# A landing margin for transfers in the planner's model, two more tiles for rows of B, one fewer for the scan states

## The chip, the cores and the metric

The kernel runs on one core of one Trainium2 chip. The metric is the device time of one execution in microseconds. The core has five engines that matter here, each with its own instruction queue, worked off in order: PE (matmuls and transposes), ACT (activations), DVE (vector operations, the scans among them), POOL (elementwise products here) and SP, which issues every transfer between memory and the on-chip buffer.

## The reference, cut to what matters

Eight images of 56 x 56 positions and 192 channels pass through two residual layers. The first is an attention with depthwise convolutions; it is the "front" of an image in the kernel, together with the convolution that opens the second layer. The second layer is a selective scan in four directions (rows and columns, each forward and backward). Its core, with A, B, C and the step size d computed from the image:

```
def step(h, inp):
    u_l, d_l, B_l, C_l = inp
    dA = jnp.exp(d_l[..., None] * A)
    dBu = d_l[..., None] * B_l[:, :, None, :] * u_l[..., None]
    h = dA * h + dBu
    y = jnp.sum(h * C_l[:, :, None, :], axis=-1)
    return (h, y)
```

There are 384 channels (three blocks of 128 partitions, NJ = 3), 16 states per channel (n = 0 to 15) and 3136 positions. The four results are added, normalized, gated and projected, and the image is added back.

## The kernel before

A *chunk* is 448 positions of one direction of one image: 7 chunks a direction, 28 a batch (an image), 224 in all. Per chunk and per state n the engines do this:

- SP loads row n of B, broadcast over 128 partitions, into a tile `bb` (L1111, L1112). The ring of such tiles has three (pool `s3`). For the states in BY_POOL it also loads the row of C into a tile `cb` (L1115), of which there are two.
- POOL multiplies `du` (step size times input, one tile for a chunk, made at L1089) by the row into a state tile `h` of 3 x 448 columns (L1126). The ring of `h` tiles has HBUFS = 8.
- ACT makes the decays `da` (L1140), one per block. DVE scans in place in `h` (L1157), three scans, and copies the last column to `newc` (L1179), from which the next chunk goes on.
- For 11 of the 16 states (13 in the last batch) PE turns `h` (L1203), ACT scales it by C on the way out (L1219), and PE turns it back and adds it up in the PSUM tile `y` (L1237). For the others POOL multiplies by the row of C (L1256), adds pairs (L1260) into the one tile `yp`, and PE adds that to `y` (L1275). DVE adds the finished `y` to the sum of directions, `yacc` (L1290, L1292).
- Before a chunk, `prepared` loads the step-size rows and the inputs and makes the step sizes `dl_s` on PE, ACT and DVE (L1066 to L1085), then `du_s` on POOL (L1089).

Beside the scan of image b run the front of image b + 1, its projections (`x_proj`) and, at the start of a batch, the `finish` of image b - 1. At that point the skip loads (L1102) refill `yacc`.

The order of the instructions on each engine is written by a planner when the program is built. Every piece of work is a generator that yields requests: an engine, a cost in us, the cells it reads and those it writes, and for a transfer a fifth number, the time from issue to landing. The class `Sched` keeps a clock for each engine, gives each time the request that can start first (less a rank), and records when its result will be there. The plan decides nothing on the chip but the order of each queue; there, an engine waits until its next instruction's inputs are there. A ring hands out its tiles in turn: `Ring.ready` says whether the next one has been released by all requests of its last user, and the last reader's planned end is taken over as the earliest time at which it may be written. Where PE would stand still by the plan for more than 2 x T_FILL, `keep_busy` puts in a small matmul on zeros (L1371, T_FILL = 0.225 us of planned time each).

The requests of a row load and of the product that uses it:

```
bb = yield s3("bb", [128, T])
yield from dma([m["k_rows"][k, c]], bb.c, 3.2, bb.ap, ...)
...
h = yield sh("h", [128, NJ, T], parts=1 + 2 * NJ)
yield POOL, t_pool(NJ * T), bb.c + du.c[1:], [h.c[0]]
nc.gpsimd.tensor_tensor(h.ap, du.ap, bb.ap.unsqueeze(1)..., ALU.mult)
```

`row_loads` is one generator: when it waits for a `cb` tile, the `bb` loads after it wait too.

Of the kernel before, what the change touches and what calls it, by code (L numbers as in the profile page):

```python
# [21 lines left out]
T = 448  # L22
# [19 lines left out]
BY_POOL = (((2, 7), (12,)), ((2, 5), (8, 10), (13,)))  # L42
EPS = 1e-5
CAP = 60.0
HBUFS = 8
LEAD = 3


# [5 lines left out]
PE, ACT, DVE, POOL, SP = range(5)  # L54
LATE = (0.17, 0.08, 0.09, 0.06, 0.0)
HOP = 0.04
URGENT = 0.4


# [104 lines left out]
class Sched:  # L164
# [37 lines left out]
    def give(self, s, t):  # L202

        e, cost, reads, writes = s.req[:4]
        end = t + cost
        self.at[e] = end
        self.used[e] += cost
        if s.group is not None and e == PE:
            self.spent[s.group] = self.spent.get(s.group, 0.0) + cost
        end = t + s.req[4] if len(s.req) > 4 else end + LATE[e]  # L210
        for c in reads:
            c.r = max(c.r, end)
        for c in writes:
            c.w = end
        s.end = max(s.end, end)
        self.resume(s)

    def run(self, until=None):
        while True:
# [20 lines left out]
            for s in self.stages:  # L240
# [3 lines left out]
                if s.group in self.limit:  # L244
# [4 lines left out]
                    if spent < must:  # L249
                        rank = URGENT  # L250
                e, _, reads, writes = s.req[:4]
# [6 lines left out]
                else:  # L258
                    for c in writes:
                        if c.r > t:  # L260
                            t = c.r
                    t = max(t + HOP, self.at[e])
                    if best is None or t - rank < best[0]:
# [9 lines left out]
def kernel(  # L273
# [93 lines left out]
    for nm, src in (("q", bn_q), ("kv", bn_kv)):  # L367
        p = load(f"bn{nm}", [CP, 4, NB], src.rearrange("v (b p) -> p v b", p=CP))
        s = const.tile([CP, NB], F32, name=f"bns{nm}")
        t = const.tile([CP, NB], F32, name=f"bnt{nm}")  # L370
# [30 lines left out]
    s3 = Rings(ctx.enter_context(tc.tile_pool(name="s3", bufs=3)), 3)  # L401
    sh = Rings(ctx.enter_context(tc.tile_pool(name="sh", bufs=HBUFS)), HBUFS)
    c1 = Rings(ctx.enter_context(tc.tile_pool(name="c1", bufs=1)), 1)
# [61 lines left out]
    def dma(reads, writes, late, dst, src, after=()):  # L465
        yield SP, 0.07, reads, writes, late
        nc.sync.dma_start(dst, src)
        for t in after:
            t.free()
# [563 lines left out]
    for i in range(2):  # L1033
        t = keep.tile([128, T], F32, name=f"dts{i}")
# [70 lines left out]
    def row_loads():  # L1105
        for i, n in todo:
            b, k, c, _ = steps[i]
            yield lambda: i in chunks
            m = made[b]
            cols = slice(c * T, (c + 1) * T)  # L1110
            bb = yield s3("bb", [128, T])  # L1111
            yield from dma([m["k_rows"][k, c]], bb.c, 3.2, bb.ap, m["rows"][k][R + n, cols].partition_broadcast(128))  # L1112
            brow[i, n] = bb
            if n in by[i]:
                cbr = yield s2("cb", [128, T])  # L1115
                yield from dma([m["k_rows"][k, c]], cbr.c, 3.2, cbr.ap,
                               m["rows"][k][R + NST + n, cols].partition_broadcast(128))
                crow[i, n] = cbr
# [178 lines left out]
    with tc.manual_schedule():  # L1297
# [11 lines left out]
        with ExitStack() as es:  # L1309
# [16 lines left out]
            for rank, g in enumerate((prepared, skips, row_loads, inputs_made, decays, scans, carries, turned, scaled,  # L1326
                                      by_pool, back, summed, evicted)):
                sc.spawn(g(), 0.3 + 0.01 * rank, "scan")
# [114 lines left out]
```

## Time and profile before

| | |
|---|---|
| median of 3 runs | 18,865.54 us (18,856.12 to 18,895.47) |
| the profiled execution: own time, span | 18,891.11 us, 18,889.4 us |
| busy share of the span | PE 90%, ACT 78%, DVE 77%, POOL 87% |
| products of du and rows of B on POOL (L1126) | 3584, 3.05 us each |
| scans on DVE (L1157) | 10,752, 1.08 to 1.14 us each |
| filler matmuls on PE (L1371) | 11,944 records, 1651 us busy |
| mean granted TensorE clock | 0.971 of full speed |

A profile is one execution. A row of it names the line of the kernel, the engine, the operation and the tiles written and read, then busy time, the mean of one, and the idle time of the engine just before these instructions with what ended it. Idle time is set down to the instruction, or the transfer, whose semaphore came last. The records of PE's matmuls are pipelined and overlap, so its busy share overstates its load. A filler matmul of the plan is two records in the profile.

### The profile page before, as it was taken

How to read it: one execution, taken by the hardware profiler on the slowest of the kernel's cores; microseconds unless marked ns; L12 is line 12 of the kernel's file. 1: busy time of each engine (PE TensorE's matmuls, PEld its weight loads, DVE VectorE, ACT ScalarE, POOL GpSimd, SP SyncE). 2: the span in 40 equal slices, each digit the busy share in tenths (PEclk: the TensorE clock that was granted, in tenths of full speed). 3: DMA queues.
4: the chain of work that ended last, by engine and by line, in shares of the span. 5: the costliest groups of instructions: out<-in, count | busy, mean ns of one | idle time of the engine just before them, and what ended most of it. 6: DMA issues, size and time to landing. Idle time of an engine off the chain costs nothing. (4 is left out here: it accounts for less than half of the span.)

```text
span 18889.4 us, 274433 instructions
## 1 busy us (share of the span) xinstructions
PE 16973.1 (90%) x96640; PEld 11599.8 (61%) x96640; DVE 14534.5 (77%) x19156; ACT 14643.6 (78%) x26598; POOL 16416.5 (87%) x7528
## 2 busy tenths in 40 slices
PE   8789998999889998899898998889988899988888
PEld 4465566666666656665666655666556665666776
DVE  2387877887778777787777877778777788778887
ACT  2378877787777878778787887878778788888888
POOL 0388998899989999899998999989999899999997
PEclk9899999999999999999999999999999999999999
DMA  1332334323333333322333333332333333342222
GB/s 52 111 89 82 96 96 120 82 85 92 104 112 84 83 95 104 112 84 81 105 100 107 83 84 101 104 106 83 83 96 110 100 83 86 100 120 76 78 78 64
DMA packets 1128347, 1750.79 MB, mean 93 GB/s; under 512 B 168516, under 2 KB 1110840, under 8 KB 1123896
## 3 DMA queue, kind: packets, MB, share of 16 engines
q1 hardware_dynamic: 1126968, 1733.23, 32.2%
q8 instruction: 764, 12.52, 0.3%
q14 instruction: 615, 5.04, 0.1%
HBM read 1545.05 MB, written 187.74 MB: 92 GB/s over the span
## 5 line engine op out<-in xcount | busy, mean ns | idle before, releaser
L1157 DVE TENSOR_TENSOR_SCAN h<-da,newc,h 128x448 f32<-128x448 f32 x9216 | 10111.4, 1136 | 2166.1 <-ACT da L1140 1155.7
L1126 POOL TENSOR_TENSOR h<-du_s,bb 128x1344 f32<-128x1344 f32 x3584 | 10836.0, 3050 | 280.5 <-DMA bb<-rows 246.0
L1140 ACT ACTIVATE da<-dl_s,acoef 128x448 f32<-128x448 f32 x10752 | 6762.2, 636 | 1149.4 <-DVE h L1157 968.0
L1219 ACT ACTIVATE g<-ht,ct_s 112x384 f32<-112x384 f32 x10080 | 5663.7, 576 | 1776.0 <-PE ht L1203 1701.2
L1237 PE MATMUL y<-ident,g 112*128 112x112 f32 x30240 | 4742.3, 271 | 660.2 <-ACT g L1219 506.3
L1237 PEld LDWEIGHTS y<-ident,g 112*128 112x128 f32 x30240 | 3305.9, 143 | 3236.8 <-ACT g L1219 2466.3
L1203 PE MATMUL ht<-ident,h 128*112 128x128 f32 x30240 | 4935.7, 277 | 287.4 <-DVE h L1157 87.4
L1203 PEld LDWEIGHTS ht<-ident,h 128*112 128x112 f32 x30240 | 3481.3, 135 | 1064.4 <-issue 450.9
L1256 POOL TENSOR_TENSOR yp<-h,cb 128x448 f32<-128x448 f32 x1932 | 2147.0, 1143 | 454.8 <-PE y L1275 216.6
L1157 DVE TENSOR_TENSOR_SCAN h<-da,h 128x448 f32<-128x448 f32 x1536 | 1598.9, 1077 | 406.0 <-ACT da L1140 214.3
L1089 POOL TENSOR_TENSOR du_s<-dl_s,du_s 128x1344 f32<-128x1344 f32 x224 | 682.6, 3047 | 1338.5 <-DVE dl_s L1085 1300.8
L1256 POOL TENSOR_TENSOR h<-h,cb 128x448 f32<-128x448 f32 x1260 | 1399.1, 1141 | 291.3 <-issue 175.6
L1371 PE MATMUL y<-zeros 128*128 128x64 f32 x11944 | 1651.3, 272 | 0.0
L1371 PEld LDWEIGHTS y<-zeros 128*128 128x128 f32 x11944 | 1586.1, 198 | 48.6 <-issue 48.6
L1275 PE MATMUL y<-yp,ident 128*128 128x448 f32 x3864 | 1594.0, 547 | 5.1 <-POOL yp L1260 4.5
L453 PE MATMUL bank<-xa,dg 128*128 128x440 f32 (+2 forms) x3024 | 1318.4, 543 | 89.0 <-ACT g L1219 52.2
L1260 POOL TENSOR_TENSOR yp<-yp,h 128x1344 f32<-128x1344 f32 x420 | 1280.9, 3050 | 1.6
L757 PE MATMUL bank<-qT,kT 128*112 128x448 f32 x2352 | 1101.8, 559 | 83.8 <-ACT pT L707 47.2
L766 PE MATMUL bank<-pT,vt 112*128 112x448 f32 x2352 | 1002.1, 546 | 66.8 <-ACT pT L707 43.4
L1275 PEld LDWEIGHTS y<-yp,ident 128*128 128x128 f32 x3864 | 701.3, 193 | 551.6 <-issue 505.2
L453 PE MATMUL bank<-band,dgq 96*96 96x440 f32 (+3 forms) x2016 | 860.9, 544 | 54.4 <-ACT hq L583 29.9
L707 ACT ACTIVATE pT<-bank,nsh 112x448 f32<-112x448 f32 x1176 | 744.3, 635 | 172.9 <-PE bank L757 152.5
(152 smaller groups left out, 12958.1 us busy)
## 6 DMA issues: line engine op xcount, KB each, us to landing
bb<-rows SPq DMA_DIRECT2D x3584, 224.0 KB
cb<-rows SPq DMA_DIRECT2D x1064, 224.0 KB
xt<-x1d SPq DMA_DIRECT2D x224, 336.0 KB
du_s<-xch SPq DMA_DIRECT2D x112, 672.0 KB
du_s<-xcw SPq DMA_DIRECT2D x112, 672.0 KB
xch<-xv SPq DMA_DIRECT2D x24, 1568.0 KB
xcw<-xw SPq DMA_DIRECT2D x168, 224.0 KB
xs<-xch SPq DMA_DIRECT2D x56, 672.0 KB
```

The costliest lines, as they stand in the source:

```text
L453: nc.tensor.matmul(out[:, o0:o1, a:b], lhs, img(lo, hi)[:, :, a + dx - 1:b + dx - 1], start=(t == TAPS[0]), stop=(t == TAPS[-1]))
L757: nc.tensor.matmul(ps.ap[:TP, :T], kts[h][:, kb * TP:(kb + 1) * TP], qh.ap, start=True, stop=True)
L1126: nc.gpsimd.tensor_tensor(h.ap, du.ap, bb.ap.unsqueeze(1).to_broadcast([128, NJ, T]), ALU.mult)
L1140: nc.scalar.activation(da.ap[:, :T], dl.ap[:, j], AF.Exp, scale=acoef[:, k * NJ + j, n:n + 1])
L1157: nc.vector.tensor_tensor_scan(h.ap[:, j, rev], da.ap[:, 0:T][:, rev], h.ap[:, j, rev], news[i - 1].ap[:, j, n:n + 1] if ci else 0.0, ALU. ...
L1203: nc.tensor.transpose(ht.ap[:TP, j * 128:(j + 1) * 128], h.ap[:, j, s * TP:(s + 1) * TP], ident)
L1219: nc.scalar.activation(g.ap, ht.ap[:TP, :DIN], AF.Copy, scale=ct.ap[:, s, n:n + 1])
L1237: nc.tensor.matmul(y["t"].ap[:, j, s * TP:(s + 1) * TP], g.ap[:, j * 128:(j + 1) * 128], ident[:TP, :TP], is_transpose=True, start=(n == 0 ...
L1256: nc.gpsimd.tensor_tensor(to.ap[:, j], h.ap[:, j], cbr.ap, ALU.mult)
L1260: nc.gpsimd.tensor_tensor(yp.ap, yp.ap, h.ap, ALU.add)
L1275: nc.tensor.matmul(y["t"].ap[:, j, :T], ident, yp.ap[:, j], start=False, stop=(y["left"][j] == 0))
L1371: nc.tensor.matmul(ybanks[:, 0, T:T + FILL], zeros, zeros[:, :FILL], start=False, stop=False)
```

## The change

A new constant, MARGIN = 3.0, is added to the planned landing of every request that has a fifth number, that is, of every transfer. The ring of `bb` tiles gets five tiles in place of three, that of `h` tiles seven in place of eight. The costs of all other requests, the ranks and the work itself stay. The lines after the constant move down by one.

```diff
-HBUFS = 8
+HBUFS = 7
...
 HOP = 0.04
+MARGIN = 3.0
 URGENT = 0.4
...
-        end = t + s.req[4] if len(s.req) > 4 else end + LATE[e]
+        end = t + s.req[4] + MARGIN if len(s.req) > 4 else end + LATE[e]
...
-            bb = yield s3("bb", [128, T])
+            bb = yield s3("bb", [128, T], 5)
```

## The prediction

> **What bounds the kernel now.** I read the page first, then the list of waits, then the line of POOL's products and POOL's timeline at a batch boundary, and last the chain.
>
> The page's first part, with the rows of POOL and of the filler:
>
> ```profile
> PE 16973.1 (90%) x96640; PEld 11599.8 (61%) x96640; DVE 14534.5 (77%) x19156; ACT 14643.6 (78%) x26598; POOL 16416.5 (87%) x7528
> ...
> L1126 POOL TENSOR_TENSOR h<-du_s,bb 128x1344 f32<-128x1344 f32 x3584 | 10836.0, 3050 | 280.5 <-DMA bb<-rows 246.0
> ...
> L1089 POOL TENSOR_TENSOR du_s<-dl_s,du_s 128x1344 f32<-128x1344 f32 x224 | 682.6, 3047 | 1338.5 <-DVE dl_s L1085 1300.8
> ...
> L1371 PE MATMUL y<-zeros 128*128 128x64 f32 x11944 | 1651.3, 272 | 0.0
> ```
>
> PE's 90% holds 1651 us of filler, so POOL is the fullest engine. A chunk of batches 0 to 6 costs it 16 products of 3.05 us, 15 of 1.14 us by rows of C, 2 sums of 3.05 and one du product of 3.05: 75.05 us. A batch is 28 x 75.05 + 7 x 3.05 (L987) = 2123 us; the trace has 2299 us between the ends of batches 2 and 3. The distances between first products of successive chunks lie from 74 to 97 us, with one of about 123 in each batch: some chunks run at POOL's floor, others do not.
>
> Who waits for whom, from the list of waits (us in total, times, longest):
>
> ```profile
> POOL du_s L1089 <- DVE dl_s L1085: 1300.8, 78, 729.9
> DVE h L1157 <- POOL h L1126: 1104.5, 489, 7.5
> ...
> POOL h L1126 <- DMA bb<-rows: 246.0, 74, 9.7
> ```
>
> and what SP's queue waits for, the longest entry:
>
> ```profile
> SPq L467 <- POOL h L1126: 9514.5, 2843, 23.7
> ```
>
> After the first 1000 us POOL idles 1652 us: 558 for du_s, 239 for a row of B, the rest mostly for scans and for yp. SP stands half the span behind a full ring of three bb tiles, and whatever is queued behind waits with it. POOL's timeline at the boundary into batch 3 shows the result:
>
> ```profile
> 7758.31 9.05 POOL L1126 TENSOR_TENSOR h<-du_s,bb 128x1344 f32<-128x1344 f32 x3
> 7774.67 3.01 POOL L1126 TENSOR_TENSOR h<-du_s,bb 128x1344 f32<-128x1344 f32 x1 [7.31 <-DMA bb<-rows]
> 7781.67 6.05 POOL L1126 TENSOR_TENSOR h<-du_s,bb 128x1344 f32<-128x1344 f32 x2 [3.99 <-DMA bb<-rows]
> ```
>
> Between the rows for n = 2 and n = 3 SP had issued seven skip loads of 672 KB, a store of the output and two of ct. But the waits of the stretch 7720 to 7850 hold little for DVE:
>
> ```profile
> POOL h L1126 <- DMA bb<-rows: 17.6, 4, 7.3
> ...
> DVE h L1157 <- POOL h L1126: 6.2, 2, 3.4
> ```
>
> DVE scans n = 3 to 8 on average 5 to 6.5 us after POOL has made them, and over all 75 waits for bb past 0.3 us (255 us) DVE's own gap before the scan concerned adds up to 9 us. The chain agrees:
>
> ```profile
> ACT 4%; DVE 4%; PE 4%; issue 1%; POOL 1%; DMA 0%; SPq 0%; POOLq 0%; ACTq 0%; DVEq 0%
> ```
>
> It reaches back only 2686 us (14%), and runs through scans, exponentials, scalings and transposes, with POOL a small part and one true bb load (6.9 us, at 16,961). So POOL is the fullest engine, but most of its waits for rows fall where it is ahead.
>
> **What the Trainium skill says.** "SBUF — State Buffer", "The DMA setup-cost knee": a transfer pays some 2 us that do not shrink with its bytes, plus bytes over 436 GB/s. For a 224 KB row load that gives an estimate of 2.5 us. From start of issue to the last landing record the trace has a median of 3.27, a mean of 3.61 and 6.5 us at the 99th percentile: longer, and the plan's 3.2 us is the median, not the tail. "DMA: Bandwidth & Descriptors", "Rules for kernel authors": issue early, wait late, and the fixed cost overlaps. That is what two more tiles allow. "Perfetto Trace Analysis", "Optimization Strategy": a bubble that repeats can mean too few buffers. The trace agrees: 7 to 9 us before n = 3 at six of the seven boundaries.
>
> **The change, part by part.** No instruction of the computation is added or removed, and the tiles take less SBUF (5376 bytes a partition off, 3584 on). The rebuilt order on the engines tells what moves; times for it come from rows of before.
>
> *Five bb tiles, and loads planned 3 us later (L1111, L210).* For each row load I took POOL's work, by its rows' durations, between the POOL instruction that lets SP go on (the product that frees the bb tile, or the product that frees a cb tile queued ahead) and the product that needs the row. Before: 818 loads have 6.2 us or less, 13 of them 3.05. After: 31 have 6.1, none less, the median goes from 9.5 to 18.7. At the boundary n = 3 and n = 4 now stand ahead of the seven skip loads. Against a mean landing of 3.6 almost all 239 us of waits should go. What it brings: with every other wait held at its measured instant, and the shortening carried along POOL to the end of its chunk, 12 us are left, since POOL then waits longer for a scan, for yp or for du_s. Counting as absorbed only what another POOL wait within 25 instructions covers leaves 125. I take -40; ends -12 and -125, and -239 if nothing absorbs it.
>
> *Seven h tiles (L45).* A tile lives from its product to the last transpose or product that reads it: 24 us in the median for a transposed one, 37 at the 90th percentile. With eight, POOL's wait for a tile is 1.5 us in all ("PE ht" under L1126). With seven at the measured instants, 178 products would start before the tile is free, by 561 us together, at n = 7, 8, 11, 13 and 14; 3.2 us each. Carried along POOL with later waits absorbing it, 112 us remain at the ends of 24 chunks. The planner knows of seven, and moves: in POOL's order a product by C at n = 10 stands one product behind its own in 121 cases for 86, and nine stand directly behind. The filler is a second measure: it is put only where the plan has PE idle, in pieces of T_FILL = 0.225; 5972 become 6180, so the plan holds 208 x 0.225 = 47 us more idle PE, from the ring and the 3 us together. What stands behind such a wait on POOL is the products by C, the sums and the next du product; DVE's scans, and ACT and PE after them, wait for POOL. I take +85; ends 0 (POOL's swaps cost nothing) and +280, half the raw overlap.
>
> *What hangs on DVE's order.* The products by C, at the mean gap of each position before and one 3.05 us product more for the nine: 720 to 728 us, +9. POOL's wait for du_s occurs where DVE's last dl step stands behind the scan of n = 15: 90 chunks before, 87 after, of 6.9 us: -20.
>
> *Filler on PE.* 1651.3 / 5972 = 0.277 us each. On the chain it is 46 of 2686 us; 3.5% more of it, scaled to the span, +11. Bounds 0 (PE idles there) and 208 x 0.277 = 58.
>
> *The 3 us on all other transfers.* The order before the first product is the same on ACT and POOL and almost so on DVE and SP, so the first 788 us stay. Waits for transfers on PE, DVE and ACT after it are 69, 34 and 24 us, 10 us at a time on xin at boundaries; the order there keeps xin behind the ct stores. I cost it at 0; the cover is that PE's next work hangs on the same bands. Bounds -60 and +40. SP issues as many transfers as before; only positions differ.
>
> Sum: -40 + 85 + 9 - 20 + 11 = +45. The profiled execution (span 18,889.4, own time 18,891.1) becomes 18,936; it lies 25.6 us above the median, to which I apply the same: 18,865.5 + 45 = **18,910**.
>
> **The rivals.** A measurement of this kernel can tell about 0.2% (38 us) from no change.
> A, the ring binds where POOL's lead is thin (forecast): 18,910, own range 18,890 to 18,990. For: at n = 10 to 15 DVE scans some 2 us behind POOL and waits 424 us for it, so a late product there passes on. Against: +47 in the plan is small.
> B, faster: the row waits are not absorbed, because the scans that POOL then waits for hang on POOL's own earlier products. -125, -20, +9, +11 and +9 for the ring: 18,750. It decides as soon as more than about 120 us of the 239 come through. For: chunks at POOL's floor have no later wait. Against: DVE's 9 us.
> C, the two cancel, or nearly all was hidden: 18,865, within 38.
> D, every release of an h tile is a wait for PE: +280 and more, 19,100 or above. For: transposes lag the scan by up to 20 us at n = 7. Against: POOL slows itself as it waits.
> That the plan would hardly differ is excluded: 75 of 224 chunks keep POOL's sequence.
>
> **How the numbers follow.** A 0.47 (0.06 of it inside 0.2%), B 0.29, C 0.16, D 0.08. Faster 0.29, same 0.22, slower 0.49. The range 18,740 to 19,050 takes A, C, the upper half of B and the bottom of D.
>
> **What would show it.** POOL's wait for bb under 40 us; a new wait of POOL's products for "PE ht" of 50 to 150 us; filler 12,360 records; du_s about as before. The forecast is wrong if the ht wait stays under 20 us, or if the wait for bb goes and the time falls by more than 60 us.

## The result, and the profile after

The changed kernel takes 18,846.83 us in the median of 20 runs (18,831.38 to 18,868.58), the kernel before 18,880.22 us in 20 runs (18,842.02 to 18,928.62). The ratio is 0.9983, 95% interval 0.9976 to 0.9989: faster by 0.17%, where 0.24% slower was forecast. The profiled execution's span is 18,837.9 us, 51.5 us less than that of the kernel before, so the two profiled executions lie somewhat farther apart than the medians (33.4 us).

The first part of the page after, and the rows that answer to those shown of before (all lines are one higher):

```profile
PE 16941.7 (90%) x97056; PEld 11613.6 (62%) x97056; DVE 14569.6 (77%) x19156; ACT 14635.9 (78%) x26598; POOL 16417.5 (87%) x7528
...
L1127 POOL TENSOR_TENSOR h<-du_s,bb 128x1344 f32<-128x1344 f32 x3584 | 10833.5, 3049 | 168.7 <-DMA bb<-rows 100.9
...
L1090 POOL TENSOR_TENSOR du_s<-dl_s,du_s 128x1344 f32<-128x1344 f32 x224 | 681.9, 3044 | 1320.8 <-DVE dl_s L1086 1281.7
L1372 PE MATMUL y<-zeros 128*128 128x64 f32 x12360 | 1706.2, 271 | 0.0
```

POOL's busy time is the same to 1 us. The idle time before the products fell from 280.5 to 168.7 us and the wait for rows of B from 246.0 to 100.9. The filler is at 12,360 records, as its count in the rebuilt order said.

The list of waits after; the numbers are the total, the times and the longest, in us:

```profile
POOL du_s L1090 <- DVE dl_s L1086: 1281.7, 70, 730.1
...
DVE h L1158 <- POOL h L1127: 929.3, 461, 7.1
...
POOL yp L1257 <- PE y L1276: 248.6, 50, 14.3
POOL yp L1257 <- issue: 222.4, 104, 7.9
...
POOL h L1257 <- DVE newc L1180: 146.9, 83, 8.0
...
POOL h L1127 <- DMA bb<-rows: 100.9, 46, 7.5
...
POOL h L1257 <- issue: 94.1, 39, 10.7
...
POOL h L1127 <- PE ht L1204: 47.1, 40, 4.3
```

The rows of the products by C in the list of before:

```profile
POOL yp L1256 <- PE y L1275: 216.6, 55, 12.9
...
POOL h L1256 <- issue: 175.6, 55, 14.7
...
POOL yp L1256 <- issue: 138.0, 75, 5.7
...
POOL h L1256 <- DVE newc L1179: 93.0, 36, 10.1
```

The last row of after is new: POOL now waits for a state tile that PE has yet to read (1.5 us before). Of the rows of L1257, the products by rows of C, three grew, the waits for y and for newc and the "issue" of yp (time in which POOL waited for nothing that the profile shows); one, the "issue" of h, fell by 81.5 us.

A sum over POOL's records tells how this adds up. In both traces, and in the eight traces of the pairs further below, the span less POOL's idle time after the first 1000 us is 17,213 to 17,242 us. POOL's work hardly changes, so **a shorter span shows up as less idle time of POOL, nearly microsecond for microsecond**. That is a way of adding up; it tells where the time went, not what caused it. POOL's idle time after the first 1000 us went from 1652 to 1610 us:

| POOL idle before, after the first 1000 us | before | after | difference |
|---|---|---|---|
| product of du and B, waiting for a row | 239 | 100 | -139 |
| the same, waiting for PE ht (a free state tile) | 1 | 47 | +46 |
| products by C and their sums | 737 | 817 | +80 |
| du product | 595 | 585 | -10 |
| the rest | 80 | 61 | -19 |
| sum | 1652 | 1610 | -42 |

The boundary into batch 3, POOL's timeline:

```profile
7756.20 18.12 POOL L1127 TENSOR_TENSOR h<-du_s,bb 128x1344 f32<-128x1344 f32 x6
7774.28 3.30 POOL L1257 TENSOR_TENSOR yp<-h,cb 128x448 f32<-128x448 f32 x3
7778.77 9.05 POOL L1127 TENSOR_TENSOR h<-du_s,bb 128x1344 f32<-128x1344 f32 x3 [1.19 <-DMA bb<-rows]
7792.16 3.04 POOL L1127 TENSOR_TENSOR h<-du_s,bb 128x1344 f32<-128x1344 f32 x1 [4.34 <-PE ht L1204]
```

Six products now stand in a row where gaps of 7.31 and 3.99 us were. Later in the same chunk the row comes 1.19 us late and a state tile 4.34 us late. The chunk's period fell from 123 to 105 us, and that of the fifth chunk after it rose from 87 to 103. The waits of 7 to 9 us before n = 3 are gone at all six boundaries that had them.

What SP waits for, after:

```profile
SPq L468 <- POOL h L1127: 5558.3, 1651, 16.7
SPq L468 <- POOL yp L1257: 2726.5, 374, 19.7
```

Before, the first was 9514.5 us, and the second was this:

```profile
SPq L467 <- POOL yp L1256: 928.1, 278, 12.8
```

With five bb tiles SP stands less behind a full ring of bb, and more behind the products by C, which give back the two cb tiles; the rows of B queued behind wait with it.

### The profile page after: what moved, and what is told of

It is laid out like the page before. It is cut to its first block, busy times and chain, and to the rows that moved or that the text cites. A ratio compares the mean times of both kernels' runs of the same rounds, so it can differ in the third digit from the quotient of the medians.

```text
span 18837.9 us, 275308 instructions
## 1 busy us (share of the span) xinstructions
PE 16941.7 (90%) x97056; PEld 11613.6 (62%) x97056; DVE 14569.6 (77%) x19156; ACT 14635.9 (78%) x26598; POOL 16417.5 (87%) x7528
## 5 line engine op out<-in xcount | busy, mean ns | idle before, releaser
L1127 POOL TENSOR_TENSOR h<-du_s,bb 128x1344 f32<-128x1344 f32 x3584 | 10833.5, 3049 | 168.7 <-DMA bb<-rows 100.9
L1257 POOL TENSOR_TENSOR yp<-h,cb 128x448 f32<-128x448 f32 x1932 | 2148.5, 1143 | 565.8 <-PE y L1276 248.6
L1372 PE MATMUL y<-zeros 128*128 128x64 f32 x12360 | 1706.2, 271 | 0.0
L1372 PEld LDWEIGHTS y<-zeros 128*128 128x128 f32 x12360 | 1635.2, 198 | 33.7 <-issue 33.7
L1257 POOL TENSOR_TENSOR h<-h,cb 128x448 f32<-128x448 f32 x1260 | 1400.5, 1143 | 260.9 <-DVE newc L1180 146.9
```

The costliest lines, as they stand in the source:

```text
L1127: nc.gpsimd.tensor_tensor(h.ap, du.ap, bb.ap.unsqueeze(1).to_broadcast([128, NJ, T]), ALU.mult)
L1257: nc.gpsimd.tensor_tensor(to.ap[:, j], h.ap[:, j], cbr.ap, ALU.mult)
L1372: nc.tensor.matmul(ybanks[:, 0, T:T + FILL], zeros, zeros[:, :FILL], start=False, stop=False)
```

## The experiments

Three accounts were set against each other. **Theory 1**: rows of B that come in time gain, the ring of seven costs. **Theory 2**: any new plan moves the time by some tenths of a per cent, and the change's 0.17% is of that kind. **Theory 3**: the idle PE time in the plan, which the filler measures, is what counts. All ratios are against the kernel before, measured beside each version.

### Each edit at the planner's own constants

Only the margin:

```diff
+MARGIN = 3.0
-        end = t + s.req[4] if len(s.req) > 4 else end + LATE[e]
+        end = t + s.req[4] + MARGIN if len(s.req) > 4 else end + LATE[e]
```

> Only the 3 us on every planned landing; three bb tiles, eight h tiles. Theory 1 (rows of B that come in time are what gains, the ring of seven costs): POOL's wait for bb falls from 246 to under 150 us since the plan no longer counts on 3.2 us, no wait for PE ht; 0.997 to 0.999 of before. Theory 2 (any new plan shifts the time by a few tenths of a per cent either way, and the change has no mechanism beyond that): anything from 0.996 to 1.004, not tied to the wait for bb. Theory 3 (the plan's idle PE time is what counts, the filler being its measure): slower by the filler it adds, up to 1.0025.

Measured: 0.9990, interval 0.9983 to 0.9996. Its rows:

```profile
L1127 POOL TENSOR_TENSOR h<-du_s,bb 128x1344 f32<-128x1344 f32 x3584 | 10844.1, 3052 | 182.0 <-DMA bb<-rows 139.6
...
L1372 PE MATMUL y<-zeros 128*128 128x64 f32 x13286 | 1821.5, 271 | 0.0
```

The wait for rows fell by 106 us with three tiles. A wait for PE ht of 23.9 us appeared, with eight state tiles, where none was expected. The plan holds 671 filler matmuls more than before (13,286 records for 11,944), 151 us of planned idle PE at 0.225 us, and the kernel is no slower. Theory 3's forecast fails: added filler is no measure of added time. That filler costs nothing is not shown, since the row waits and the clock (see below) changed with it.

Only the shorter ring of states:

```diff
-HBUFS = 8
+HBUFS = 7
```

> Only seven h tiles in place of eight. Theory 1: POOL gains a wait for PE ht of 30 to 100 us and keeps the 246 us for bb: 1.002 to 1.005. Theory 2: 0.996 to 1.004 with no such tie. Theory 3: slower as far as filler rises.

Measured: 1.0000, interval 0.9992 to 1.0008. From its list of waits:

```profile
POOL h L1126 <- DMA bb<-rows: 231.1, 66, 10.3
...
POOL h L1126 <- PE ht L1203: 8.5, 6, 6.3
```

Seven tiles cost nothing that this measurement can tell. POOL waits 8.5 us for a state tile, where 30 to 100 were expected and +85 us of time was forecast for the ring.

Both rings without the margin (five bb tiles and eight h tiles do not fit the buffer together: 25.75 KB a partition are wanted for the front's pool and 22.94 left, so five tiles alone were not tried):

```diff
-HBUFS = 8
+HBUFS = 7
-            bb = yield s3("bb", [128, T])
+            bb = yield s3("bb", [128, T], 5)
```

> Five bb tiles and seven h tiles, planned landings as before. Theory 1: the wait for bb falls to 50 to 120 us from the tiles alone, the wait for ht is some 50 us: 0.998 to 1.000. If it stands where the changed kernel stands (0.998), the margin did nothing. Theory 2: 0.996 to 1.004.

Measured: 0.9971, interval 0.9961 to 0.9982: faster than with the margin added.

```profile
POOL h L1256 <- DVE newc L1179: 286.7, 83, 11.4
POOL h L1126 <- DMA bb<-rows: 75.4, 37, 5.9
POOL h L1126 <- PE ht L1203: 48.8, 7, 8.5
```

The two rings without the margin take the wait for rows to 75 us. The wait of the products by C for newc went the other way, 93.0 to 286.7; other waits of these products fell, so that in all (with their sums) they idle 789 us after the first 1000, for 737 before.

The margin and seven h tiles, three bb tiles (the first and the second edit together):

> The 3 us and seven h tiles, three bb tiles. Theory 1: without the two tiles most of the gain is missing: wait for bb 100 to 200 us, wait for ht some 50 us: 0.999 to 1.003. Theory 2: 0.996 to 1.004, whatever these waits do.

Measured: 0.9963, interval 0.9950 to 0.9975, the best of the four and 0.27% below the margin alone, so the shorter ring again cost no time. Its two waits:

```profile
POOL h L1127 <- DMA bb<-rows: 142.6, 63, 9.4
POOL h L1127 <- PE ht L1204: 58.8, 19, 9.2
```

Neither wait explains its place. That spoke for Theory 2, and the next runs measured how far a plan moves by itself.

### The same kernels under other plans

One constant of the planner was changed, HOP, which it adds as a hand-over between engines. No tile, transfer or request is treated otherwise; the plan only falls out differently:

```diff
-HOP = 0.04
+HOP = 0.045
```

The kernel before:

> The kernel before with HOP 0.045 in place of 0.04 in the planner: no tile and no transfer is treated differently, only the ties and near-ties of the plan fall differently. Theory 2 (any new plan shifts the time by some tenths of a per cent): 0.996 to 1.004, and its distance from 1 is a sample of that size. Theory 1 (the gains come from rows of B that are there in time): 1.000 within 0.1%, POOL's wait for bb 220 to 260 us.

The changed kernel:

> The changed kernel (3 us, five bb, seven h) with HOP 0.045. Theory 1: stays at 0.998 within 0.1%, wait for bb about 100 us. Theory 2: 0.995 to 1.002, and as likely better as worse than 0.998.

The two rings without the margin:

> Five bb and seven h tiles without the 3 us, HOP 0.045. Theory 1: stays at 0.997 within 0.1%, wait for bb about 70 us; then the margin costs 0.1% on top of the tiles. Theory 2: 0.995 to 1.001.

The margin with seven h tiles:

> The 3 us and seven h tiles with three bb tiles, HOP 0.045. Theory 1 has no reason why this was the best of all (0.9963), since its wait for bb was 140 us; Theory 2 expects it to fall back to some 0.998. If it stays at 0.996, the three tiles with the margin are better than five for a reason still to be found.

Then the kernel before and the changed kernel with HOP 0.03:

> The kernel before with HOP 0.03: a third plan of the same resources. Theory 2 (the change's 0.17% is within what any new plan does): a third value in 0.994 to 1.004, not tied to the wait for bb. Theory 1 (rows in time gain): 1.000 within 0.1% as for HOP 0.04.

> The changed kernel with HOP 0.03, to be set against the kernel before with HOP 0.03. Theory 1: faster than that by 0.1 to 0.3%. Theory 2: the difference of the pair has either sign, up to 0.5%. In both: the wait for bb is less than half of its partner's, and a wait for ht of 30 to 80 us appears.

and with HOP 0.05:

> The kernel before with HOP 0.05: a fourth plan. Theory 2: 0.994 to 1.004. A further possibility: a larger HOP is nearer to the chip's own delay, so that 0.045 was no luck; then this one is at 0.996 or below as well.

> The changed kernel with HOP 0.05, to be set against the kernel before with HOP 0.05. Theory 1: faster than that by 0.1 to 0.3%. Theory 2: either sign, up to 0.5%.

The two parts with HOP 0.03 and 0.05:

> Five bb and seven h tiles without the margin, HOP 0.03 (before at 0.03: 1.0072, all three edits: 1.0015). If the tiles carry the gain: 1.001 to 1.004, wait for bb under 140 us. If the margin carries it: 1.006 to 1.009.

> The margin and seven h tiles with three bb tiles, HOP 0.03. If the margin carries the gain: 1.001 to 1.004 or below, as at 0.04 and 0.045 where it was the best. If the tiles carry it: 1.005 to 1.009. Wait for bb 100 to 180 us.

> Five bb and seven h tiles without the margin, HOP 0.05 (before at 0.05: 0.9929, all three edits: 0.9882). If the tiles carry the gain: 0.988 to 0.991. If the margin carries it: 0.992 to 0.995.

> The margin and seven h tiles with three bb tiles, HOP 0.05. If the margin carries the gain: 0.985 to 0.990. If the tiles carry it: 0.991 to 0.995.

and the pair with HOP 0.08:

> The kernel before with HOP 0.08. If a larger HOP gains because the plan's hand-over between engines was too short: 0.985 to 0.993. If the order of 0.03 to 0.05 was chance: anything from 0.993 to 1.005.

> The changed kernel with HOP 0.08, to be set against the kernel before with HOP 0.08. If the three edits gain through rows of B that are there in time: faster than that by 0.2 to 0.6%, wait for bb lower by 100 us or more. If chance of the plan decides: the wait for bb is lower all the same, the time of either sign.

Measured, ratios to the kernel before as it was (HOP 0.04); the intervals are 0.0014 to each side or less, and 0.0017 and 0.0015 for the two at 0.08:

| | HOP 0.03 | 0.04 | 0.045 | 0.05 | 0.08 |
|---|---|---|---|---|---|
| the kernel before | 1.0072 | 1 | 0.9960 | 0.9929 | 0.9901 |
| all three edits (the change) | 1.0015 | 0.9983 | 0.9964 | 0.9882 | 0.9894 |
| two rings, no margin | 1.0059 | 0.9971 | 0.9989 | 0.9958 | |
| margin and seven h tiles | 0.9976 | 0.9963 | 0.9915 | 1.0029 | |
| the change over before, same HOP | 0.994 | 0.998 | 1.000 | 0.995 | 0.999 |
| two rings over before, same HOP | 0.999 | 0.997 | 1.003 | 1.003 | |
| margin and seven over before, same HOP | 0.990 | 0.996 | 0.995 | 1.010 | |

The lower three rows are quotients of the upper ones. What follows from them:

- A plan alone moves this kernel by more than the change did: the kernel before spans 1.7%. Chance alone is not likely to be all of that: its five values fall with HOP without exception. That the larger hand-over is nearer to what the chip takes was only argued; where it stops gaining was not tried.
- The change is clearly faster than its partner in three of five pairs, by 0.17 to 0.6%; in the other two (1.0004 at 0.045, 0.9993 at 0.08) the difference is within the intervals. The mean of the five quotients is 0.9975. Theory 1's 0.1 to 0.3% in every pair did not hold, nor did Theory 2's "either sign": no pair shows a loss beyond its intervals.
- The parts show no such rule. Both have quotients on both sides of one. That the margin with seven tiles is the better version, as three plans had it, is refuted by the plan at 0.05. Both parts at 0.05 lay outside both of the ranges expected for them.

What holds in all five pairs is that the wait for rows falls. POOL's rows of products, the kernel before and the changed kernel at HOP 0.045, where the times are equal:

```profile
L1126 POOL TENSOR_TENSOR h<-du_s,bb 128x1344 f32<-128x1344 f32 x3584 | 10841.2, 3051 | 209.8 <-DMA bb<-rows 166.1
L1256 POOL TENSOR_TENSOR yp<-h,cb 128x448 f32<-128x448 f32 x1932 | 2149.0, 1144 | 366.8 <-PE y L1275 162.7
```

```profile
L1127 POOL TENSOR_TENSOR h<-du_s,bb 128x1344 f32<-128x1344 f32 x3584 | 10840.2, 3052 | 147.7 <-PE ht L1204 80.1
L1257 POOL TENSOR_TENSOR yp<-h,cb 128x448 f32<-128x448 f32 x1932 | 2152.1, 1147 | 456.5 <-PE y L1276 214.4
```

The idle time before the products of du fell by 62 us, that before the products into yp rose by 90. And at HOP 0.05, where the change gained most among the better plans:

```profile
L1126 POOL TENSOR_TENSOR h<-du_s,bb 128x1344 f32<-128x1344 f32 x3584 | 10839.6, 3051 | 202.9 <-DMA bb<-rows 164.5
L1256 POOL TENSOR_TENSOR yp<-h,cb 128x448 f32<-128x448 f32 x1932 | 2146.6, 1143 | 410.1 <-issue 110.3
```

```profile
L1127 POOL TENSOR_TENSOR h<-du_s,bb 128x1344 f32<-128x1344 f32 x3584 | 10837.1, 3051 | 97.1 <-DMA bb<-rows 47.3
L1257 POOL TENSOR_TENSOR yp<-h,cb 128x448 f32<-128x448 f32 x1932 | 2150.2, 1145 | 421.8 <-PE y L1276 199.0
```

Here 106 us went at the products and only 12 came back before yp. For all pairs, POOL's idle time in us after the first 1000, the kernel before and the changed one:

| HOP | waiting for a row | waiting for PE ht | products by C and sums | du product | all idle |
|---|---|---|---|---|---|
| 0.03 | 250, 114 | 27, 18 | 811, 782 | 638, 686 | 1801, 1672 |
| 0.04 | 239, 100 | 1, 47 | 737, 817 | 595, 585 | 1652, 1610 |
| 0.045 | 167, 44 | 7, 80 | 693, 782 | 614, 558 | 1560, 1560 |
| 0.05 | 164, 48 | 9, 22 | 684, 743 | 603, 545 | 1533, 1430 |
| 0.08 | 174, 52 | 3, 9 | 495, 681 | 686, 617 | 1453, 1441 |

The row wait falls by 116 to 139 us in each pair, 127 in the mean. The idle time in all falls by 0 to 129, 57 in the mean: in sum more than half of what went at the rows came back elsewhere, most often before the products by C, and how much depends on the plan. These are differences of sums. That the later waits grew because the row waits went is the likely reading, not shown.

The fastest kernel measured is the changed one with HOP 0.05: 18,662.34 us, 0.9882 (0.9869 to 0.9895). With HOP 0.08 the kernel before is at 0.9901 and the changed one at 0.9894, so most of a gain of that size can be had by HOP without the change.

### A rival that no run settles: the clock of PE

The profile also records the clock that PE was granted. In these traces it has two values, full and half. In the profiled executions PE stood at half for 1095 us before and for 896 after. The mean granted clock over the runs of each kernel, as a share of full speed:

| | HOP 0.03 | 0.04 | 0.045 | 0.05 | 0.08 |
|---|---|---|---|---|---|
| the kernel before | 0.9722 | 0.9716 | 0.9746 | 0.9740 | 0.9742 |
| all three edits (the change) | 0.9762 | 0.9760 | 0.9748 | 0.9770 | 0.9752 |
| two rings, no margin | 0.9728 | 0.9722 | 0.9725 | 0.9746 | |
| margin and seven h tiles | 0.9790 | 0.9784 | 0.9800 | 0.9747 | |

The margin alone had 0.9783. So in all ten comparisons of a kernel with the margin against the kernel before at the same HOP the mean clock was higher, if only by 0.0002 for the change at 0.045. In the seven where it rose by 0.003 or more the time fell, by 0.1 to 1.0%. In the three where it rose by 0.001 or less it did not fall beyond the intervals: the change at 0.045 and at 0.08, and the margin with seven h tiles at 0.05, which was 1.0% slower. In the first two of these the wait for rows fell by 123 and 122 us, as far as in the other pairs, and the time stayed.

In 108 runs of the kernel before, beside the experiments, a run with 0.001 more clock was about 13 us shorter (correlation -0.66, within the five sets in which they ran). By that slope the change's 0.0044 goes with an estimated 57 us, more than the 33 measured. This shows no direction: a run that waits less may also hold the full clock longer. Nor is the clock everything, since the two rings at 0.04 gained 0.29% with 0.0006 more of it. But no run holds the clock fixed while the rows change, so how much of the gain comes from rows that are there in time is open.

## Why the prediction was wrong

**The ring of seven, +85.** This is the term that failed. The two numbers under it were 112 us, from holding before's instants and order, and 47, from the filler. Seven tiles alone measured 1.0000, within 0.0008 (15 us), and POOL's new wait was 8.5 us. In the full change it was 47 us, just under the 50 to 150 named as its mark. Nor is that wait the ring's alone: with eight tiles it was 23.9 us with the margin and 27.1 us in the kernel before at HOP 0.03. The likely reason is the one that the prediction named with an end of 0: the planner knows the ring and moves other work of POOL in front, which arithmetic with a fixed order leaves out. The prediction took a value between its two estimates instead. Neither of its two signs of being wrong occurred (a wait for PE ht under 20 us, or a fall of more than 60 us); only the run with seven tiles alone shows that this term failed.

**The filler as a measure of the plan, +47 us within that term, and +11 on PE.** The margin alone has 671 filler matmuls more and measured 0.9990, so added filler did not go with added time. A possible reason, not shown: with a margin the plan has PE wait for transfers that on the chip have landed, and fills time that is not idle there.

**The rows of B, -40.** The traces fit the mechanism: the waits go, and others of POOL grow. The size was of the right order: -139 at the rows and +80 at the products by C, and in the pairs POOL's idle time falls by 57 us where the row waits fall by 127. That is in part luck, since -40 was a choice between 12 and 125. The mark "under 40 us" was missed (100.9). The count of POOL's work between release and use assumed landings of 3.6 us; with five tiles in flight they took 4.26 in the mean, and SP now stands 2726 us behind products by C. Which of the two left the 101 us was not tested.

**The du wait, -20, and the products by C, +9.** The first was about as forecast (-10). The second was +80. The likely reason is that the mean gap for each position was taken from before, where POOL had come late to those products because it had waited for rows.

**What was not in the sum** is, first, the clock of PE, which had no term: it rose from 0.9716 to 0.9760, as worked out above. Second, it is the spread of plans: 0.3 to 0.7% in the kernel before for a step of 0.005 to 0.01 in a constant that the change does not touch. POOL's sequence differs in 149 of 224 chunks; the prediction costed the parts that could be named and gave the rest of the new order no width of its own. The forecast of a sign had less ground than its chances said: rival B's mechanism (waits not absorbed) and A's (a wait for PE ht) are both in the trace, 139 against 46 us, and their balance changed with each plan. Rival D, where POOL waits for PE at every release, did not occur. The measured time lies where rival C stood: its number came true, a fall of 0.17%, inside the band of 0.2% that was called "same". Of its account, row waits balanced by the ring, only a part is in the trace (46 us); the products by C took more (80).

What stays open: what shares of the gain the rows and the clock have; why three plans favoured the margin with seven h tiles and three bb tiles (0.4 to 1.0%) and one opposed it by 1%; and whether the mean gain of the five pairs would hold over many more plans.

## What to carry to other kernels

Where a planner writes the order, an edit to its inputs is judged over several plans that differ in something that the edit does not touch; here one pair of plans could not tell 0.2%. Waits that go at one place of the fullest engine can come back at its next ones: here 127 us less at the rows went with 57 us less idle time in all. A ring's length should not be priced with the old order kept, and idle time and filler of the plan should not be read as time on the chip. Where the granted clock differs between two versions, that difference belongs in the comparison, beside the waits.

## What the runs showed of the hardware that was not expected

A row load takes longer to land with five bb tiles than with three. From the start of issue to the last of a load's landing records the median over 3584 loads was 3.27 us before, 3.18 with the margin alone and 3.19 with seven h tiles alone, all with three bb tiles; with five it was 3.99 without the margin and 4.23 with it, and 3.98 to 4.02 in the changed kernel at the other four values of HOP. The tail is less clear: the 99th percentile was 6.50 us before and 8.35 after, but already 7.02 with the margin alone and 7.32 in the kernel before at HOP 0.03. That more loads are under way at once is the likely reason; it was not counted. The tiles that let a load start earlier give part of that back as a longer flight.
